# Two-layer decoder on one core: TensorE in place of DMA for the transpose of the attention weights, and three smaller re-orderings

## The chip, the cores and the metric

The kernel runs on one core of a Trainium2 chip. The metric is the device time of one execution in microseconds (us). TensorE (PE), VectorE (DVE), ScalarE (ACT), GpSimd (POOL) and SyncE (SP) each work through their own list of instructions in order and wait for each other by semaphores. SP only starts DMA transfers here. Matmul results land in PSUM, which the kernel divides into eight banks of 512 f32 values for each partition; DVE and ACT read them there.

## The reference, cut to what matters

Sixteen sequences of 128 tokens with 256 features (2048 rows in all) go through two decoder layers. Each layer is attention, cross attention and a feed-forward part, each with a residual and a layer norm.

```
x = layernorm(x + L0_attn(x))          # 16 heads of 128: local window and top-8 of compressed keys, out @ Wo + bo
x = layernorm(x + L0_xattn(x, ctx))    # 16 heads of 16, 2048 queries by 2048 keys, quantised
x = layernorm(x + L0_ffn(x))           # silu(gate) * up, 256 -> 1024 -> 256
x = layernorm(x + L1_attn(x))          # 32 heads of 8, causal inside a block of 128
x = layernorm(x + L1_xattn(x, ctx))    # 16 heads of 16, own sequence's context
x = layernorm(x + L1_ffn(x))           # 16 experts, top 6, and a shared expert

# L0_xattn, after the scores
attn = softmax(q @ k.T)                              # all 2048 keys of all sequences
attn = round(attn / (max/255)) clipped to 0..255     # an unsigned byte for each weight
out  = attn @ v @ Wp + bp
```

In the first attention the values have a bias: `lv = x @ Wlv + blv`, and the merged context is halved before `@ Wo`.

## The kernel before, in words

The stages run one after the other. By the profiled execution the first attention takes from the start to about 806 us, the preparation of the first cross attention to 879, its main loop (with the feed-forward part of the layer woven in) to 1618 and its tail to 1674, the second layer's attention to 1968, its cross attention to 2192, the experts to the end.

**First attention.** Steps are (block of 128 tokens, group of four heads), 64 in all, software-pipelined over four iterations: `normed` and `values` project (L355), `transposed` and `scores` follow one iteration later, `weightsT` two, `contexts` (L467) and `output` three. PE's order is written out by hand; a scheduler orders DVE, ACT and POOL. `contexts` ends with one ACT copy of four heads (L474, `mT`, scale 0.5). The bias `blv` is not added to the values: `output_bias` (L492), called once at n == 6, multiplies half of it by `Wo` with 16 matmuls of broadcast columns (POOL copies L497, PE L498), adds that to `bo` and adds `bo` to all 16 tiles `xs` (POOL, L501). SP loads the four `xT` groups first (L66), then `wcmp`, the tables, the weights, and the tiles `x` last.

**First cross attention.** A group `gp` is two query tiles, and a step is (gp, pair of heads i, tile u): 128 steps, 16 to a group, each of two parts. All engines are in an order written by hand. In each part PE makes the scores of 1024 keys for both heads (`scores`, L759, two tiles `s` of two banks from three buffers), DVE scales each and keeps the running maximum (`scaled`, L774, 128x1024 from PSUM). One step later ACT turns 2048 scores of one head into bytes with one exponential (`weights8`, L795; `snl` of L786 is its bias). The bytes are viewed as 16-bit words, and a DMA transpose on SP's queue (L803) brings the keys to the partitions. Two steps later POOL spreads the bytes to bf16 (`spread`, L807), and three to four steps later PE multiplies them with the values `vq` (`context`, L817). Because a word holds two keys, `values_by_key` (L651) lays the values out in the same order of two.

Beside it, `pair_work` and `due` place the queries of the next group (`query`; `query_cols` is a DMA transpose, L611), the division, the output projection, and the feed-forward part of the previous group: in steps 8 to 15 of a group the gate and up products (`ffn_gate`, L889), on ACT `ffn_out` (L907, L908) and `ffn_sigmoid` (L911).

**Second layer's attention.** Steps are (tile t, half c of the heads, quarter e), 64 in all; PE's order is written by hand. Keys of four heads are masked into one tile `kz` (POOL, L1253); `attend_scores` adds the causal mask with bf16 matmuls (L1261), then two products of 32 rows each, which lie in different row groups of PE (L1265), into one of two buffers `sc` of two banks; DVE takes the maximum (L1274) and subtracts it (L1276), ACT exponentiates (L1277). Two steps later PE transposes the weights (L1285) and ACT copies them (L1286); three steps later come the contexts (L1295) and the division (L1305). The projections (L1379), the values (L1388) and the output (L1324) share one PSUM tile `misc`.

Of the kernel before, what the change touches and what calls it, by code (L numbers as in the profile page):

```python
# [27 lines left out]
P = 128  # L28
# [20 lines left out]
def decoder(ctx: ExitStack, tc: tile.TileContext, w: dict, out: bass.AP):  # L49
# [15 lines left out]
    for g in range(NG):  # L65
        nc.sync.dma_start(out=xT[g], in_=xT_dram[:, :, g * G : (g + 1) * G])  # L66
# [125 lines left out]
    with ExitStack() as ph:  # L192
# [5 lines left out]
        nc.sync.dma_start(out=wcmp, in_=w["L0_attn_Wcmp"].rearrange("(k p) n -> p k n", p=P))  # L198
        rope_t = pool.tile([P, 4, 32], F32, name="rope_t")
# [23 lines left out]
        bo = load_row(pool, w["L0_attn_bo"], "bo0")  # L223
        for t in range(NB):
            nc.sync.dma_start(out=xs[t], in_=w["x"][t * P : (t + 1) * P, :])
# [241 lines left out]
        def contexts(b, st):  # L467

            pm = ps.tile([P, 4, P], F32, tag="pm", name="pm", bufs=1)
            for h in range(4):  # L470
                nc.tensor.matmul(pm[:, h, :], lhsT=st["Wlv"][:, h, :], rhs=st["plT"][:, h, :], start=True, stop=False)
                nc.tensor.matmul(pm[:, h, :], lhsT=cvz[b % 3][:, h, :], rhs=st["pcT"], start=False, stop=True)
            st["mT"] = wk.tile([P, 4, P], F32, tag="mT", name="mT")
            nc.scalar.activation(st["mT"], pm, AF.Copy, scale=0.5)  # L474
# [16 lines left out]

        def output_bias():  # L492

            pb = ps.tile([P, HID], F32, tag="po", name="pb", bufs=1)
            for h in range(NH):
                rep = wk.tile([P, P], F32, tag="blv_b", name="blv_b")
                nc.gpsimd.tensor_copy(rep, blv[:, h : h + 1].to_broadcast([P, P]))  # L497
                nc.tensor.matmul(pb, lhsT=rep, rhs=wts["Wo", h // 4][:, h % 4, :], start=h == 0, stop=h == NH - 1)  # L498
            nc.vector.scalar_tensor_tensor(bo, pb, 0.5, bo, ALU.mult, ALU.add)
            for t in range(NB):  # L500
                nc.gpsimd.tensor_tensor(xs[t], xs[t], bo, ALU.add)  # L501
# [7 lines left out]
        with tc.manual_schedule(engines={mybir.EngineType.PE}):  # L509
# [4 lines left out]
            for n in range(len(steps) + 6):  # L514
# [5 lines left out]
                if fourth:  # L520
                    contexts(fourth[0], fourth[2])
# [14 lines left out]
                if n == 6:  # L536
                    output_bias()
# [32 lines left out]
    with ExitStack() as ph:  # L570
# [40 lines left out]
        def query_cols(t):  # L611
            nc.sync.dma_start_transpose(out=qT[t % 4].bitcast(U16), in_=rows3.rearrange("p h d -> p (h d)").bitcast(U16))

        qs = {}
        with tc.tile_pool(name="l0x_1", bufs=1) as p1, tc.tile_pool(name="l0x_p0", bufs=2, space=PSUM) as ps0:
# [35 lines left out]
            def values_by_key(t4):  # L651
                pt = ps0.tile([P, 4, 2, P], BF16, tag="pt3", name="ptv")
                for i in range(4):
                    for c in range(2):
                        at = t4 * G + (i // 2) * 2 * P
                        keys = vqT[:, c, at : at + 2 * P].rearrange("p (w j) -> p j w", j=2)
                        nc.tensor.transpose(pt[:, i, c, :], keys[:, i % 2, :], ident16)
                nc.scalar.copy(vq[:, 4 * t4 : 4 * t4 + 4, :].rearrange("p t (c d) -> p t c d", c=2), pt)
# [49 lines left out]
            for n in range(NB + 4):  # L708
# [15 lines left out]
                if n in (7, 10):  # L724
                    query_cols(n // 10)
# [33 lines left out]
        def scores(gp, i, u, half, st):  # L759

            t = 2 * gp + u
            s = [ps.tile([P, 2, G], F32, tag="s", name="s", bufs=3) for _ in range(2)]
            for c in range(2):
                at = (2 * half + c) * G
                for hh in range(2):
                    r = slice(64 * hh, 64 * hh + 64)
                    nc.tensor.matmul(  # L767
                        s[hh][:, c, :], lhsT=qT[t % 4][r, i, :], rhs=kT[r, i, at : at + G], start=True, stop=True
                    )
            return s  # L770
# [17 lines left out]
        def weights8(gp, i, u, hh, st):  # L788
# [5 lines left out]
            a = wk.tile([P, 2 * G], U16, tag="a", name="a", bufs=3)  # L794
# [7 lines left out]
            at = wk.tile([P, 8, P], U16, tag="at", name="at", bufs=4)  # L802
            nc.sync.dma_start_transpose(out=at, in_=a)  # L803
            st["at"].append(at)

        def spread(u, hh, st, aT):
            nc.gpsimd.tensor_copy(  # L807
                aT[:, :, hh, u * P : (u + 1) * P].rearrange("p (b j) q -> p b j q", j=2),
                st["at"][hh].bitcast(U8).rearrange("p b (q j) -> p b j q", j=2),
            )  # L810
# [70 lines left out]
        def ffn_gate(q, i, n, tag="misc"):  # L881

            if n == 0:
                pp = ps.tile([P, 2, G] if tag == "s" else [P, 2, 2 * P], F32, tag=tag, name="gu", bufs=3 if tag == "s" else 1)
# [32 lines left out]
        def ffn_down_psum(tag="misc"):  # L917
            pp = ps.tile([P, 2, G] if tag == "s" else [P, G], F32, tag=tag, name="pd", bufs=3 if tag == "s" else 1)
# [30 lines left out]
        def query(t, at):  # L949
# [14 lines left out]
            later(at + 5, "SP", query_cols, t)  # L964
# [99 lines left out]
        ordered = [getattr(mybir.EngineType, nm) for nm in ("PE", "DVE", "Activation", "Pool", "SP")]  # L1064
        with tc.manual_schedule(engines=set(ordered)):
            for n in range(len(steps) + 9):
                now = steps[n] if n < len(steps) else None
                if now is not None:
                    if n % 16 == 0:
                        group(n // 16)  # L1070
                    if n < NB:
# [4 lines left out]
                        "at": [],  # L1076
                    }
                for part in range(2):
                    at = 2 * n + part
                    if now is not None:  # L1080
                        s = scores(*now, part, states[n])
                        scaled(*now, part, 0, states[n], s)
                        due(at, "DVE")
                        scaled(*now, part, 1, states[n], s)
                    else:
                        due(at, "DVE")
# [41 lines left out]
                    due(at, "SP")  # L1128
# [10 lines left out]
                states.pop(n - 2, None)  # L1139
# [116 lines left out]
    def attend_scores(wk, psum, qT, kz, blocks, mask):  # L1256

        sc = psum.tile([P, 2, 4, P], F32, tag="sc", name="sc", bufs=2)
        if mask is not None:
            for b in range(2):  # L1260
                nc.tensor.matmul(  # L1261
                    sc[:, b].rearrange("p j k -> p (j k)"), lhsT=ident16, rhs=mask, start=True, stop=False
                )
        for b, r in enumerate(blocks):
            nc.tensor.matmul(  # L1265
                sc[:, b].rearrange("p j k -> p (j k)"),
                lhsT=qT[r],
                rhs=kz[r].rearrange("p j k -> p (j k)"),
                start=mask is None,
                stop=True,  # L1270
            )
        sc = sc.rearrange("p b j k -> p (b j) k")
        mx = stat.tile([P, 8], F32, tag="amx", name="amx")
        nc.vector.tensor_reduce(mx, sc, AX.X, ALU.max)  # L1274
        pr = wk.tile([P, 8, P], F32, tag="pr", name="pr", bufs=3)
# [79 lines left out]
    with ExitStack() as ph:  # L1355
# [15 lines left out]
        cross_load()  # L1371
        moe_load()
        vs, qkT = {}, {}

        def project_a(g, n, c):

            pp = ps.tile([P, G], F32, tag="misc", name="proj")
# [16 lines left out]
        steps = [(t, c, e) for t in range(NB) for c in range(2) for e in range(2)]  # L1394
        kzs, prs, prTs, oTs = {}, {}, {}, {}
        with tc.manual_schedule(engines={mybir.EngineType.PE}):
            for n in range(2):
                for c in range(2):
                    project_a(0, n, c)
            values_a(0)  # L1400
            for n in range(len(steps) + 16):
                if n == 4:
                    cross_tables()

                if n in (5, 7):
                    q = NB // 2 - 2 + n // 7
                    norm_pair_xT(q, norm_pair_T(q, ps, "misc"))
                if n < len(steps):
                    t, c, e = steps[n]
                    cols = slice((t % 4) * P, (t % 4 + 1) * P)  # L1410
                    if e == 0:
                        kzs[c] = masked_keys(wk, qkT[t // 4, 1, c][:, cols], own1)
                    blocks = [slice(32 * i, 32 * i + 32) for i in (2 * e, 2 * e + 1)]
                    prs[n] = attend_scores(
                        wk, ps, qkT[t // 4, 0, c][:, cols], kzs[c], blocks, causal.rearrange("p j k -> p (j k)")
                    )
                if 0 <= n - 3 < len(steps):
                    t, c, e = steps[n - 3]
                    if e == 1:
                        attend_context([prTs.pop(n - 4), prTs.pop(n - 3)], vs[t], ones1, o2[:, c], 16 * c)  # L1420
                        oTs[t, c] = attend_divide(wk, o2[:, c])
                if 0 <= n - 2 < len(steps):
                    prTs[n - 2] = attend_transpose(wk, ps, prs.pop(n - 2))
                t, r = n // 4, n % 4
                if r == 0 and t // 4 + 1 < NG:
                    project_a(t // 4 + 1, t % 4 // 2, t % 2)
                elif r == 1 and t + 1 < NB:
                    values_a(t + 1)
                elif r == 3 and 0 <= t - 1 < NB:
                    attend_output(ps, t - 1, [oTs.pop((t - 1, c)) for c in range(2)], wz)  # L1430
                    if t % 4 == 0:
                        norm(t // 4 - 1)
                elif r == 2 and t // 4 >= 1 and t % 4 in (1, 2):
                    norm_T(t // 4 - 1, t % 4 - 1, ps, "misc")
# [4 lines left out]
    with ExitStack() as ph:  # L1439
# [51 lines left out]
        with tc.manual_schedule(engines={mybir.EngineType.PE}):  # L1491
# [8 lines left out]
            for n in range(len(steps) + 14):  # L1500
                if n < len(steps):
# [4 lines left out]
                    prs[n] = attend_scores(wk, ps, cols[t, 0][:, c, :], kzs.pop((t, c)), blocks, None)  # L1506
# [145 lines left out]
```

## Time and profile before

| | us |
|---|---|
| median of three runs (lowest, highest) | 2724.48 (2720.74, 2729.77) |
| the profiled execution's own time | 2727.17 |
| its span, first to last instruction | 2725.2 |
| outside the span | 2.0 |
| PE, DVE, ACT, POOL busy in the span | 2519.4, 1903.5, 1472.8, 1215.8 |
| first attention, 60 to 645: PE, DVE, ACT, POOL busy of 585 | 578.5, 453.0, 317.4, 288.2 |
| first cross attention, 878 to 1616: the same of 738 | 653.0, 688.9, 621.7, 618.9 |
| second layer's attention, 1676 to 1970: the same of 294 | 281.5, 212.5, 154.8, 90.1 |

Busy times of PE include the time in which results run out of its pipeline, so that a busy PE is not yet a full one. [...] In a row such as `L795 ACT ACTIVATE a<-e,snl ... x256 | 510.8, 1996 | 3.5` the numbers are the total busy time, the mean of one in nanoseconds, and the idle time of the engine just ahead of these instructions.

### The profile page before, as it was taken

To read this page: it belongs to the slowest core of one execution; us is meant where nothing else is said; L and a number is where in the kernel's file an instruction comes from. 1 tells how busy PE (TensorE), PEld (TensorE's weight loads), DVE (VectorE), ACT (ScalarE), POOL (GpSimd) and SP (SyncE) were. 2 spreads that over 40 slices of the span, in tenths; PEclk is the share of its full clock that TensorE was granted. 3 is DMA by queue.
4 is the path that set the end of the run, shared out by engine and by line. 5 is a ranking of instruction groups with operands and counts; after the bars stand their busy time and mean duration, and the time that the engine had idled before them with its cause. 6 is when DMAs were issued, how large, how long until landed. Compare 5 with 4: busy or idle time off the path is not lost. (4 is left out here: it accounts for less than half of the span.)

```text
span 2725.2 us, 39543 instructions
## 1 busy us (share of the span) xinstructions
PE 2519.4 (92%) x13877; PEld 1494.7 (55%) x13908; DVE 1903.5 (70%) x4365; ACT 1472.8 (54%) x2778; POOL 1215.8 (45%) x1336
## 2 busy tenths in 40 slices
PE   6999999999997788988988898999988899999998
PEld 3677777777764123433433345666655546564746
DVE  5677777877757999989999973777777742324232
ACT  3455555555543888977987873555554531313120
POOL 5544544444436888878888883223132200000000
PEclk9999999999998799999999999999999999999999
DMA  8000000000010566665665563100100011112120
GB/s 252 1 1 1 1 1 1 1 1 1 1 39 13 103 111 119 128 111 115 124 124 107 112 141 94 59 2 2 44 15 11 2 66 43 54 39 61 33 67 10
DMA packets 360150, 150.69 MB, mean 55 GB/s; under 512 B 294576, under 2 KB 341136, under 8 KB 359440
## 3 DMA queue, kind: packets, MB, share of 16 engines
q1 hardware_dynamic: 358592, 144.49, 22.9%
q0 software_dynamic: 1360, 3.68, 0.6%
q8 instruction: 110, 1.80, 0.3%
q14 instruction: 88, 0.72, 0.1%
HBM read 74.57 MB, written 2.23 MB: 28 GB/s over the span
## 5 line engine op out<-in xcount | busy, mean ns | idle before, releaser
L807 POOL CAST aT<-at 128x2048 bf16<-128x2048 uint8 x256 | 481.2, 1894 | 88.9 <-DMA at<-a 83.0
L795 ACT ACTIVATE a<-e,snl 128x2048 uint8<-128x2048 f32 x256 | 510.8, 1996 | 3.5
L774 DVE TENSOR_SCALAR_CACHE_REDUCE e<-s,qs,smx 128x1024 f32<-128x1024 f32 x256 | 335.2, 1335 | 14.7 <-PE s L767 13.9
L774 DVE TENSOR_SCALAR_CACHE_REDUCE e<-s,qs 128x1024 f32<-128x1024 f32 x256 | 319.9, 1281 | 33.8 <-PE s L767 28.8
L817 PE MATMUL o<-aT,vq 128*32 128x512 bf16 x1024 | 266.3, 395 | 3.3 <-POOL aT L807 3.3
L767 PE MATMUL s<-kT,qT 64*128 64x512 bf16 x1024 | 189.8, 399 | 30.0 <-DVE e L774 27.1
L1564 DVE TENSOR_TENSOR h<-h,up 128x512 f32<-128x512 f32 (+1 forms) x100 | 68.8, 688 | 192.4 <-PE up L1560 191.0
L1563 ACT ACTIVATE h<-gate 128x512 f32<-128x512 f32 (+1 forms) x100 | 59.7, 597 | 220.5 <-PE gate L1560 220.2
L817 PEld LDWEIGHTS <-vq 128*32 128x32 bf16 x1024 | 86.2, 98 | 165.5 <-issue 91.8
L1560 PE MATMUL gate<-xT,w_L_ffn_w1g 128*128 128x512 f32 x352 | 167.7, 595 | 0.0
L1560 PE MATMUL up<-xT,w_L_ffn_w1u 128*128 128x512 f32 x352 | 165.4, 592 | 0.0
L1274 DVE TENSOR_REDUCE amx<-sc 128x8 f32<-128x1024 f32 x96 | 116.7, 1216 | 62.4 <-PE sc L1265 62.2
L1591 PE MATMUL py<-w_L_ffn_w2T,h 128*128 128x256 f32 x704 | 154.6, 379 | 0.0
L1277 ACT ACTIVATE pr<-pr 128x1024 f32<-128x1024 f32 x96 | 101.6, 1059 | 88.3 <-DVE pr L1276 88.3
L1286 ACT COPY prT<-tp 128x512 f32<-128x512 f32 x192 | 104.3, 584 | 76.9 <-PE tp L1285 76.5
L1591 PEld LDWEIGHTS py<-w_L_ffn_w2T,h 128*128 128x128 f32 x704 | 133.7, 190 | 18.3
L889 PE MATMUL gu<-xT,wgu 128*128 128x256 f32 x448 | 132.3, 419 | 9.6 <-ACT gu_s L908 4.9
L425 ACT ACTIVATE pls<-sc,lm,rms_rs 128x128 f32<-128x128 f32 x256 | 113.8, 454 | 21.7 <-DVE lm L421 21.7
L355 PE MATMUL proj<-Wlk,xT 128*128 128x512 f32 x256 | 121.5, 597 | 3.0 <-ACT raw_Wlv L381 1.8
L482 PE MATMUL po<-Wo,mT 128*128 128x256 f32 x512 | 121.2, 380 | 1.4 <-ACT mT L474 1.4
L355 PE MATMUL proj<-Wq,xT 128*128 128x512 f32 x256 | 122.3, 601 | 0.2 <-DVE raw_Wlk L364 0.2
L1276 DVE TENSOR_TENSOR pr<-sc,amx 128x1024 f32<-128x1024 f32 x96 | 117.0, 1219 | 5.7
(313 smaller groups left out, 5383.5 us busy)
## 6 DMA issues: line engine op xcount, KB each, us to landing
wgu<-in_L_ffn_gu SPq DMA_DIRECT2D x112, 128.0 KB
sh<-share SPq DMA_DIRECT2D x32, 256.0 KB
at<-a SPq DMA_TRANSPOSE x256
sh<-share SPq DMA_DIRECT2D x16, 224.0 KB
sh<-share SPq DMA_DIRECT2D x16, 192.0 KB
w_L_ffn_w1g<-in_L_ffn_w1g SPq DMA_DIRECT2D x1, 2816.0 KB
w_L_ffn_w1u<-in_L_ffn_w1u SPq DMA_DIRECT2D x1, 2816.0 KB
w_L_ffn_w2T<-in_L_ffn_w2T SPq DMA_DIRECT2D x1, 2816.0 KB
```

Source lines behind the costliest of these rows:

```text
L355: nc.tensor.matmul(pp.rearrange("p h d -> p (h d)"), lhsT=xTt(b, k), rhs=wts[nm, hg][:, k, :], start=k == 0, stop=k == 1)
L482: nc.tensor.matmul(outs[b], lhsT=st["mT"][:, h, :], rhs=wts["Wo", hg][:, h, :], start=hg == 0 and h == 0, stop=hg == 3 and h == 3,)
L767: nc.tensor.matmul(s[hh][:, c, :], lhsT=qT[t % 4][r, i, :], rhs=kT[r, i, at : at + G], start=True, stop=True)
L774: nc.vector.tensor_scalar(st["e"][hh][:, half, :], s[hh].rearrange("p a b -> p (a b)"), qs[2 * gp + u][:, 2 * i + hh : 2 * i + hh + 1], No ...
L795: nc.scalar.activation(a.bitcast(U8), st["e"][hh].rearrange("p a b -> p (a b)"), AF.Exp, bias=st["nm"][:, hh : hh + 1], accum_out=groups[g ...
L807: nc.gpsimd.tensor_copy(aT[:, :, hh, u * P : (u + 1) * P].rearrange("p (b j) q -> p b j q", j=2), st["at"][hh].bitcast(U8).rearrange("p b ...
L817: nc.tensor.matmul(o[r : r + 32].rearrange("p a b -> p (a b)"), lhsT=vq[:, n, 32 * i : 32 * i + 32], rhs=aT[:, n].rearrange("p a b -> p (a ...
L889: nc.tensor.matmul(ffn_ps[q][:, n, :], lhsT=wt[:, k, :], rhs=xT[q // 2][:, k, at], start=k == 0, stop=k == 1)
L1274: nc.vector.tensor_reduce(mx, sc, AX.X, ALU.max)
L1276: nc.vector.tensor_tensor(pr, sc, bc(mx, 2, P), ALU.subtract)
L1560: nc.tensor.matmul(pp[:rows], lhsT=wt[:, k, :], rhs=xT[g][:, k, :], start=k == 0, stop=k == 1)
L1591: nc.tensor.matmul(py, lhsT=h[:rows, i4 * P : (i4 + 1) * P], rhs=wt, start=n == 0, stop=n == len(parts) - 1)
```

## The change

1. **Weights' words by TensorE.** `weights8` writes its bytes into a tile seen as 512 words of 32 bits. `words_T` transposes four blocks of 128 words on PE into PSUM, and `words_out` copies them to SBUF as 1024 elements of 16 bits: ACT does it, but for the first parts of steps 8 to 15 of a group, where DVE does it. `spread` and `values_by_key` now count four keys to a word. The scores' tiles `s` have two buffers in place of three; two banks go to the transposes. `query_cols` becomes eight PE transposes and an ACT copy.
2. **First attention.** Only `xT[0]` is loaded early, right after `wcmp`; the other three come after the weights and before `x`. `output_bias` is gone: ACT adds half of `blv` in the copies `mT`, one copy for each head, and POOL adds `bo` to each tile `x`.
3. **Second layer's attention.** A step is a half tile: four mask matmuls, then four products of 32 rows in four row groups, into both buffers `sc`; the order on ACT is written by hand too. The loads for the next stages are issued one step into the loop, and the first projections take the two transposes' buffers.

```diff
-    for g in range(NG):
+    def load_xT(g):
         nc.sync.dma_start(out=xT[g], in_=xT_dram[:, :, g * G : (g + 1) * G])
...
         nc.sync.dma_start(out=wcmp, in_=w["L0_attn_Wcmp"].rearrange("(k p) n -> p k n", p=P))
+        load_xT(0)
...
         bo = load_row(pool, w["L0_attn_bo"], "bo0")
+        for g in range(1, NG):
+            load_xT(g)
...
-            nc.scalar.activation(st["mT"], pm, AF.Copy, scale=0.5)
+            for h in range(4):
+                n = 4 * hg + h
+                nc.scalar.activation(st["mT"][:, h, :], pm[:, h, :], AF.Identity, bias=blv[:, n : n + 1], scale=0.5)
...
-                if n == 6:
-                    output_bias()
+                if n == 2:
+                    nc.vector.tensor_scalar_mul(blv, blv, 0.5)
+                if n % 4 == 2 and n // 4 < NB:
+                    nc.gpsimd.tensor_tensor(xs[n // 4], xs[n // 4], bo, ALU.add)
...
-            s = [ps.tile([P, 2, G], F32, tag="s", name="s", bufs=3) for _ in range(2)]
+            s = [ps.tile([P, 2, G], F32, tag="s", name="s", bufs=2) for _ in range(2)]
...
-            a = wk.tile([P, 2 * G], U16, tag="a", name="a", bufs=3)
+            a = wk.tile([P, G], F32, tag="a", name="a", bufs=4)
...
-            at = wk.tile([P, 8, P], U16, tag="at", name="at", bufs=4)
-            nc.sync.dma_start_transpose(out=at, in_=a)
-            st["at"].append(at)
+            st["a"].append(a)
+
+        def words_T(hh, st):
+            pt = ps.tile([P, 4, P], F32, tag="tp", name="aTp", bufs=2)
+            for b in range(4):
+                nc.tensor.transpose(pt[:, b, :], st["a"][hh][:, b * P : (b + 1) * P], ident)
+            return pt
+
+        def words_out(hh, st, pt, copy):
+            at = wk.tile([P, 4, P], F32, tag="at", name="at", bufs=3)
+            copy(at.bitcast(U16), pt.bitcast(U16))
+            st["at"][hh] = at
...
                     if now is not None:
                         s = scores(*now, part, states[n])
-                        scaled(*now, part, 0, states[n], s)
-                        due(at, "DVE")
-                        scaled(*now, part, 1, states[n], s)
-                    else:
-                        due(at, "DVE")
+                        for hh in range(2):
+                            scaled(*now, part, hh, states[n], s)
+                    due(at, "DVE")
+
+                    m = n - 2 + part
+                    if 0 <= m < len(steps):
+                        on_dve = m % 16 >= 8 and part == 0
+                        pt = words_T(1 - part, states[m])
+                        words_out(1 - part, states[m], pt, nc.vector.tensor_copy if on_dve else nc.scalar.copy)
+                    due(at, "PE")
...
-            later(at + 5, "SP", query_cols, t)
+            later(at + 5, "PE", lambda: box.update(T=query_cols(ps, "tp")))
+            later(at + 6, "ACT first", lambda: nc.scalar.copy(qT[t % 4], box["T"]))
...
+        scs = [psum.tile([P, 2, 4, P], F32, tag="sc", name="sc", bufs=2) for _ in range(len(blocks) // 2)]
+        banks = [sc[:, b].rearrange("p j k -> p (j k)") for sc in scs for b in range(2)]
         if mask is not None:
+            for bank in banks:
+                nc.tensor.matmul(bank, lhsT=ident16, rhs=mask, start=True, stop=False)
+        for bank, r in zip(banks, blocks):
...
+                if 0 < h < len(halves):
+                    scs = half_scores(t, c)
...
+                if 0 <= h - 2 < len(halves):
+                    u, d = halves[h - 2]
+                    attend_context([prTs.pop((h - 2, e)) for e in range(2)], vs[u], ones1, o2[:, d], 16 * d)
+                for e in range(2):
+                    if 0 <= h - 1 < len(halves):
+                        prTs[h - 1, e] = attend_transpose(wk, ps, prs.pop((h - 1, e)))
+                if h < len(halves):
+                    for e in range(2):
+                        prs[h, e] = attend_exp(wk, scs[e], 4)
```

## The prediction

> **What bounds the kernel now.** I read the page first, then the busy time of each engine by stage, then the groups of instructions, then the timeline of one step in each changed stage. The profiled execution took 2727.17 us, span 2725.2; it lies 2.7 above the median of the three runs, and my sum is made against 2727.
>
> PE is busy everywhere, but that is an average over stages with different limits.
>
> ```profile
> span 2725.2 us, 39543 instructions
> PE 2519.4 (92%) x13877; PEld 1494.7 (55%) x13908; DVE 1903.5 (70%) x4365; ACT 1472.8 (54%) x2778; POOL 1215.8 (45%) x1336
> ```
>
> In the first attention PE hardly waits: 578 of 585 us busy. In the loop of the first cross attention (879 to 1618, 738 us, 128 steps of 5.77) the stretches of one group each look like this (columns: stretch, its length, then busy time and instructions of PE, PEld, DVE, ACT, POOL, granted clock, DMA share, GB/s):
>
> ```profile
> 1155.00:1247.00 92.00, 83.28 (x372) 36.22 (x369) 83.48 (x141) 76.32 (x106) 75.96 (x67) 0.94 0.60 115
> 1247.00:1340.00 93.00, 84.60 (x384) 36.65 (x382) 86.44 (x147) 78.17 (x106) 79.62 (x71) 0.96 0.59 119
> ```
>
> Four engines at 82 to 93%: DVE is nearest to full, ACT has 15 us of 92 free. Steps 8 to 15 of a group, with the feed-forward work, take 5.36 us each, ACT back to back; steps 0 to 7 take 6.2. The groups that pay:
>
> ```profile
> L795 ACT ACTIVATE a<-e,snl 128x2048 uint8<-128x2048 f32 x256 | 510.8, 1996 | 3.5
> L774 DVE TENSOR_SCALAR_CACHE_REDUCE e<-s,qs,smx 128x1024 f32<-128x1024 f32 x256 | 335.2, 1335 | 14.7 <-PE s L767 13.9
> L774 DVE TENSOR_SCALAR_CACHE_REDUCE e<-s,qs 128x1024 f32<-128x1024 f32 x256 | 319.9, 1281 | 33.8 <-PE s L767 28.8 <-ACT snl L786 3.0 <-ACT gu_s L908 1.3
> L1276 DVE TENSOR_TENSOR pr<-sc,amx 128x1024 f32<-128x1024 f32 x96 | 117.0, 1219 | 5.7
> L706 ACT COPY kT<-pt 128x1024 bf16<-128x1024 bf16 x16 | 16.2, 1012 | 26.1 <-PE pt L705 26.1
> ```
>
> And the timeline, where I take hand-over times from (start, length, engine, line):
>
> ```profile
> 101.38 7.82 PE L498 MATMUL pb<-Wo,blv_b 128*128 128x256 f32 x28 [0.20 <-POOL blv_b L497]
> 109.74 11.75 POOL L501 TENSOR_TENSOR x<-x,bo 128x256 f32<-128x256 f32 x16 [1.30 <-DVE bo L499]
> 130.43 0.49 PE L471 MATMUL pm<-plT,raw_Wlv 128*128 128x128 f32 x2 [1.40 <-ACT plT L461]
> 132.54 0.49 PE L472 MATMUL pm<-pcT,cvz 128*128 128x128 f32 x2 [1.63 <-DVE pcT L465]
> ...
> 1198.34 2.00 ACT L795 ACTIVATE a<-e,snl 128x2048 uint8<-128x2048 f32 x1
> 1200.49 1.23 SPq L803 DMA_TRANSPOSE at<-a  x1
> ...
> 1804.20 0.86 PEld L1285 LDWEIGHTS tp<-ident,pr 128*128 128x128 f32 x8 [0.76 <-ACT prT L1286]
> 1804.89 1.07 ACT L1286 COPY prT<-tp 128x512 f32<-128x512 f32 x2 [0.31 <-PE tp L1285]
> ...
> 1815.49 0.59 PE L1261 MATMUL sc<-causal,ident 128*128 128x512 bf16 x2
> 1816.02 1.13 PE L1265 MATMUL sc<-kz,qkT 32*128 32x512 f32 x4
> 1817.07 1.08 PE L1295 MATMUL o<-prT,vz 128*32 128x128 f32 x32
> ```
>
> **The loop, on ACT.** The transposes leave SP's queue, where they cost no engine; 192 of 256 copies of 1024 16-bit elements come to ACT and 64 to DVE. The price is row L706, the same shape from PSUM: 1.01, and 0.98 from start to start. More than the copies counts their place. ACT's list is now copy, exponential, copy, exponential, and each copy needs the PE transpose of the exponential just before it. The chain of a part: from the start of an exponential until its bytes are released 2.13 (887.12 to 889.23 and 1198.34 to 1200.49), four transposes until ACT may start 0.70 (1804.20 to 1804.89), copy 0.98. Sum 3.81 for a part, 7.62 for a step. `snl` (0.30) fits in the wait of 0.8. In steps 0 to 7 both copies are ACT's: 61.0, and between copy and exponential two query copies (0.98) and copies of `ot` and `xT` (0.47 each): 63.9. In steps 8 to 15 one copy is DVE's: 2.13 + 0.70 + 0.98 + exponential 2.00 + the two reads of `gu` 0.73 + `snl` 0.33 = 6.87.
>
> **The loop, on DVE and PE.** With three buffers PE wrote half of the next scores while DVE still read. With two, the second head's tile is free only when DVE has done both: each part costs DVE's two readings and then PE's remaining products. The readings take 2.50 and 2.62 a part (1206.25 to 1208.75, 1208.93 to 1211.55); then 0.14 until PE starts (886.56 to 886.69), 0.64 from the scores to DVE (1218.92 to 1219.56): 0.78. A step is 5.12 + 1.56 = 6.68. In steps 8 to 15 DVE's copy fills one such gap. No 16-bit copy by DVE from PSUM is in the trace; the nearest rows, 1024 elements from PSUM, take 1.22 to 1.28, a copy of 128 takes 0.27. Between these I take 1.22, the row of that size: 6.68 + 0.44 = 7.12, longer than ACT's 6.87. The other end lies under the gap of 0.78 and leaves ACT's 6.87. In steps 0 to 7 DVE's other work (about 1.0 a step) sits in the gaps and ACT's 7.62 decides. PE's own work: eight transposes of 0.108 add 0.9 to about 4.5 a step, below either chain; but they stand in order ahead of the feed-forward and context products, which now wait for ACT with them. POOL's bytes come with another stride; I keep 1.89 (L807), two a step plus 1.5 of feed-forward, 5.3 of 7.
>
> Sum of a group: 63.9 + 8 x 7.12 = 120.9, before 92.2: +28.7, eight groups +229; the first group has less beside it: **+226**. Bounds: ACT's own instructions without a wait give steps of 6.29 with DVE's 6.68 over them, 53.4 + 57.0 a group, +146; all waits one behind the other, 8.2 a step (below), +335. I take the chain, as its order is fixed.
>
> Two rules of the Trainium skill can be weighed here. The rows price 1024 elements from PSUM at 1.22 on DVE; "VectorE: DVE Perf Modes", section "Why PSUM operands drop a tier", lets 16-bit data from PSUM run at two a cycle, an estimate of 0.66 by its table of costs; steps 8 to 15 would then take 6.87 and the sum would be 16 less. The rows show PE waiting only 27 us for DVE in this loop with three buffers; "Perfetto Trace Analysis", section "Matmuls", wants independent groups to rotate through banks so that the emptying of one overlaps the next, which speaks against the step from three to two: without that loss the sum would be smaller by the same 16, as ACT's chain stays.
>
> **First attention.** `output_bias` held PE from 98.95 to 109.03: -10.1. Its 16 additions kept POOL to 121.5, and PE lost 5.3 behind it (1.40, 1.63, and matmuls at half pace until 136): gone from there. At the start, PE now waits for 0.5 MB in place of 2 MB: in the trace `wcmp` came at 18.7, and 12 us of work lie from `lg` (23.4) to the next projection (35.5). By bytes at the measured 285 GB/s I expect a lead of 12.5. But the scheduler now puts the additions of `bo` on POOL in the third step, and they wait there for the tiles `x`, which land last: 14.1 of 17.1 MB, at about 49.5. Behind them stand `raw_Wlk` of that step and the next. POOL then needs 16 x 0.73 between its other work, until about 67, where PE's transposes would have been at 58.6: lead left 3 (0 to 12.5). The four `mT` copies cost ACT at most 4 x 0.454 (L425) against 0.59; PE needs them 2.6 after the contexts (59.68 to 62.28) and ACT is 54% busy: nothing, but 0.7 twice at the end, where nothing covers it. Sum **-18** (-8 to -28).
>
> **Second layer's attention.** PE sets the pace, 17.3 a tile. The scores of a quarter are 0.53 + 1.05, a half 3.16; four products side by side with four masks 0.95 + 1.05 = 2.00: -1.16. But the eight blocks of each quarter are now transposed in a row, four PSUM tiles from two buffers: the third waits for the first copy (0.70 + 0.58 + 0.1), so 2.35 in place of 1.72: +0.63. DVE is below: 4.96 for a half, 1.25 division, 0.5, and 1.8 until the next scores. A tile: 2 x -0.53 = -1.06, sixteen tiles -17; the first projections no longer share one buffer (1677.06 to 1685.09): -5. Sum **-22**. If the four products ran two by two, 2 x (-0.11 + 0.63) x 16 = +17 - 5 = +12; at DVE's pace of 14 a tile, -53.
>
> Total: 2727 + 226 - 18 - 22 = 2913, rounded to **2910**.
>
> **Rivals.**
> - *The wait is hidden.* PE's transpose overtakes, and ACT is held by its own work alone: +146 in the loop, 2833. For it: two PSUM buffers and four of `a`. Against: one list, one order.
> - *The waits add up.* In steps 8 to 15 PE stands at the scores for DVE and only then takes the words ACT waits for: 3.1 from scores to scores, 0.70, 0.98, then 2.00 + 0.73 + 0.33 and hand-overs, 8.2; the same in steps 0 to 7 with the extra copies: +335, about 3020. For it: PE is in order. Against: DVE's and ACT's cycles settle side by side when neither waits for the other's late half.
> - *Two by two.* The four products do not run together: 34 more, 2944.
> - *Not slower.* The DMA traffic (60% of the loop) is what held its engines, and they run faster without it. The loop must then take 778 at most, 6.08 a step: it decides from a chain shorter by 20%. Priced at that, 2720. Against: all 256 exponentials lie between 1985 and 2011 ns, with the queue full or empty, and DVE waits for PE, not for data.
>
> **How the numbers follow.** Forecast 0.58 (2850 to 2975), hidden 0.17, adding up 0.13, two by two 0.09, not slower 0.03. About 0.3% (8 us) is what a measurement can tell from no change. The range, 2825 to 2990, takes in most of the second and fourth case. Faster 0.03, same 0.01, slower 0.96.
>
> **What the profile after would show.** Right: the step near 7.6 in the first half of a group and 7.1 in the second; idle time of ACT ahead of the word copy, released by PE; that copy near 1.01; PE waiting for DVE ahead of the scores, several times the 27 us; `x` additions on POOL waiting for DMA at 45 to 55 us; the tile of the second layer's attention near 16.2. Wrong: ACT copies near 0.6, DVE or POOL fuller than ACT, or a stage outside these three that moves.

## The result, and the profile after

The changed kernel takes 2978.41 us (median of four runs, 2973.44 to 2978.68), before 2722.89. The ratio is 1.0929, with a 95% interval of 1.0906 to 1.0953. The predicted time was 2910, its range 2825 to 2990. The profiled execution's span grew from 2725.2 to 2976.6, by 251.4. From the traces' starts of a few instructions it splits like this:

| stretch | before | after | difference |
|---|---|---|---|
| start to the first exponential of the cross attention | 887.1 | 875.6 | -11.6 |
| first to last exponential of the loop | 733.9 | 995.8 | +261.9 |
| from there to the second layer's first projection | 56.1 | 59.1 | +3.0 |
| second layer's attention, to the first scores of its cross attention | 302.6 | 298.0 | -4.6 |
| the rest | 745.5 | 748.2 | +2.7 |

So the loop lost 265 with its drain, and the two small parts gave 16. On the page of the kernel after, PE, DVE and POOL have lost share, and ACT went only from 54% to 57%, though the work of ACT (+226) and PE (+151) grew much:

```profile
span 2976.6 us, 41945 instructions
PE 2670.3 (90%) x15028; PEld 1610.8 (54%) x15028; DVE 1950.6 (66%) x4429; ACT 1698.4 (57%) x3178; POOL 1212.8 (41%) x1320
```

The third and the fifth group of 16 steps, to be set beside the two stretches of before (columns: stretch, its length, busy time and instructions of PE, PEld, DVE, ACT, POOL, granted clock, DMA share, GB/s):

```profile
1120.80:1246.00 125.20, 104.39 (x533) 51.55 (x533) 93.14 (x157) 103.87 (x134) 80.83 (x71) 0.99 0.06 18
1373.50:1499.30 125.80, 105.78 (x533) 51.91 (x533) 93.11 (x157) 103.87 (x134) 80.81 (x71) 0.97 0.06 17
```

A group takes 125 in place of 92. DVE was busy 83 of 92 and 86 of 93 us; now it is busy 93 of 125. No engine is above about 84%, and the DMA share fell from 0.60 to 0.06. As nothing is full, I looked for a chain of waits. The groups of instructions say which one (idle time ahead of each, and its releasers, last):

```profile
L795 ACT ACTIVATE a<-e,snl 128x2048 uint8<-128x2048 f32 x256 | 513.6, 2006 | 1.9
L774 DVE TENSOR_SCALAR_CACHE_REDUCE e<-s,qs 128x1024 f32<-128x1024 f32 x256 | 318.8, 1282 | 171.1 <-PE s L767 152.1
L774 DVE TENSOR_SCALAR_CACHE_REDUCE e<-s,qs,smx 128x1024 f32<-128x1024 f32 x256 | 333.6, 1341 | 91.3 <-PE s L767 91.3
L813 ACT COPY at<-aTp 128x1024 uint16<-128x1024 uint16 x192 | 194.3, 1012 | 176.0 <-PE aTp L807 167.4
L807 PE MATMUL aTp<-ident,a 128*128 128x128 f32 x1024 | 177.5, 298 | 106.5 <-ACT a L795 106.1
L767 PE MATMUL s<-kT,qT 64*128 64x512 bf16 x1024 | 193.4, 398 | 31.7 <-DVE e L774 30.3
```

ACT's wait stands ahead of the word copy (176.0), hardly ahead of the exponential (1.9); its releaser is PE's transpose, and where PE waits ahead of the transposes (106.5), the releaser is the exponential just before. DVE waits 243 us for PE's scores, before 43. The timeline of ACT in steps 0 to 7 of a group shows the bare beat:

```profile
1251.30 2.00 ACT L795 ACTIVATE a<-e,snl 128x2048 uint8<-128x2048 f32 x1
1253.29 0.28 ACT L786 ACTIVATE snl<-smx,ln 128x2 f32<-128x2 f32 x1
1254.19 1.01 ACT L813 COPY at<-aTp 128x1024 uint16<-128x1024 uint16 x1 [0.62 <-PE aTp L807]
1255.10 2.00 ACT L795 ACTIVATE a<-e,snl 128x2048 uint8<-128x2048 f32 x1
1257.99 1.01 ACT L813 COPY at<-aTp 128x1024 uint16<-128x1024 uint16 x1 [0.80 <-PE aTp L807]
1258.90 2.00 ACT L795 ACTIVATE a<-e,snl 128x2048 uint8<-128x2048 f32 x1
```

From 1251.30 to 1258.90 two parts in a row (the second of step 0 and the first of step 1) take 7.60, where the forecast chain is 7.62. That it fits this closely is partly luck: from an exponential to its copy are 2.89 (1255.10 to 1257.99) against 2.83, from the copy to the next exponential 0.91 against 0.98. And it accounts for a step only when PE comes in time. The next part, on PE:

```profile
1257.25 0.66 PE L807 MATMUL aTp<-ident,a 128*128 128x128 f32 x4 [0.47 <-ACT a L795]
1257.74 0.61 PE L612 MATMUL ptq<-ident,rows 128*128 128x128 bf16 x8
1258.28 1.47 PE L827 MATMUL o<-aT,vq 128*32 128x512 bf16 x6
1259.68 1.56 PE L934 MATMUL pd<-w_L_ffn_d,h 128*128 128x256 f32 x6
1261.17 0.61 PE L767 MATMUL s<-kT,qT 64*128 64x512 bf16 x4
1261.71 0.66 PE L807 MATMUL aTp<-ident,a 128*128 128x128 f32 x4
```

ACT's exponential of 1258.90 was over at about 1261.0. Its transposes start at 1261.71, because query rows, contexts, a down product and the next scores stand ahead of them in PE's order. In groups 1 to 6, 42 of the 48 steps 0 to 7 take 8.1 to 10.5, one 7.8, and only five 7.6.

### The profile page after: what moved, and what is told of

It is laid out like the page before. It is cut to its first block, busy times and chain, and to the rows that moved or that the text cites. A ratio compares the mean times of both kernels' runs of the same rounds, so it can differ in the third digit from the quotient of the medians.

```text
span 2976.6 us, 41945 instructions
## 1 busy us (share of the span) xinstructions
PE 2670.3 (90%) x15028; PEld 1610.8 (54%) x15028; DVE 1950.6 (66%) x4429; ACT 1698.4 (57%) x3178; POOL 1212.8 (41%) x1320
## 3 DMA queue, kind: packets, MB, share of 16 engines
q8 instruction: 119, 1.95, 0.3%
## 5 line engine op out<-in xcount | busy, mean ns | idle before, releaser
L795 ACT ACTIVATE a<-e,snl 128x2048 uint8<-128x2048 f32 x256 | 513.6, 2006 | 1.9
L813 ACT COPY at<-aTp 128x1024 uint16<-128x1024 uint16 x192 | 194.3, 1012 | 176.0 <-PE aTp L807 167.4
L807 PE MATMUL aTp<-ident,a 128*128 128x128 f32 x1024 | 177.5, 298 | 106.5 <-ACT a L795 106.1
L807 PEld LDWEIGHTS aTp<-ident,a 128*128 128x128 f32 x1024 | 113.7, 147 | 234.5 <-ACT a L795 201.7
L1265 POOL TENSOR_TENSOR vz<-v,ones 128x1024 f32<-128x1024 f32 (+1 forms) x32 | 58.4, 1826 | 202.0 <-ACT v L1402 83.3
L899 PE MATMUL gu<-xT,wgu 128*128 128x256 f32 x448 | 124.7, 402 | 13.8 <-ACT xT L161 11.5
```

The costliest lines, as they stand in the source:

```text
L795: nc.scalar.activation(a.bitcast(U8), st["e"][hh].rearrange("p a b -> p (a b)"), AF.Exp, bias=st["nm"][:, hh : hh + 1], accum_out=groups[g ...
L807: nc.tensor.transpose(pt[:, b, :], st["a"][hh][:, b * P : (b + 1) * P], ident)
L813: copy(at.bitcast(U16), pt.bitcast(U16))
L899: nc.tensor.matmul(ffn_ps[q][:, n, :], lhsT=wt[:, k, :], rhs=xT[q // 2][:, k, at], start=k == 0, stop=k == 1)
```

## The experiments

All figures by group are means over the groups 1 to 6 of the loop, from the starts of the exponentials: before 49.3 for steps 0 to 7 and 43.9 for steps 8 to 15, after 70.0 and 55.5. Where "one run" is said, the kernel has a single time, so that differences under 10 us between such kernels are not read.

### The loop of before with the two small parts

```diff
-            s = [ps.tile([P, 2, G], F32, tag="s", name="s", bufs=2) for _ in range(2)]
+            s = [ps.tile([P, 2, G], F32, tag="s", name="s", bufs=3) for _ in range(2)]
...
-        def words_T(hh, st):
...
+            nc.sync.dma_start_transpose(out=at, in_=a)
+            st["at"].append(at)
...
```

> The changed kernel with the first cross attention of before (DMA transposes of words and query rows, three buffers s), the other two parts kept. My theory, from the profile after: the loop and its drain cost 264 of the 251 by which the span grew, the first attention gives 10.9 and the second layer's attention 4.7. This kernel should take 2727 - 11 - 5 = about 2711 by the profiled execution, 2704 to 2716. Rival 1: part of the 264 comes from the other two parts (the moved loads, another fill of the loop); then it stays at or above 2720. Rival 2: the small parts give what was forecast, 18 and 22; then about 2687.

Measured: 2709.03 against 2723.82, ratio 0.9948 (0.9932 to 0.9964). The gain is 15, the 16 of the stretches and not the forecast 40. The small parts are worth what their stretches show, and all of the loss lies in the loop.

### Two buffers for the scores, and nothing else

```diff
-            s = [ps.tile([P, 2, G], F32, tag="s", name="s", bufs=3) for _ in range(2)]
+            s = [ps.tile([P, 2, G], F32, tag="s", name="s", bufs=2) for _ in range(2)]
```

> The kernel before with two buffers s in place of three and nothing else changed (two banks lie idle). By the sum of the prediction each part costs DVE's two readings and 0.78 until the next scores: 6.68 a step in place of 5.36 in steps 8 to 15 and of 6.2 in steps 0 to 7, the loop at least 855 in place of 738, the total about 2840 (2820 to 2860). Rival: PE waited only 27 us for DVE in this loop, and the scores come early enough with two buffers: 0 to 20 more, 2725 to 2745.

One run: 2860.11, so +136, at the upper end of what was expected. Half of the loop's loss needs no transpose and no copy. The groups of DVE and of PE's scores in this run (idle time was 14.7 and 33.8 before on DVE, and PE waited 27 for DVE):

```profile
L774 DVE TENSOR_SCALAR_CACHE_REDUCE e<-s,qs,smx 128x1024 f32<-128x1024 f32 x256 | 335.4, 1336 | 72.9 <-PE s L767 72.9
L774 DVE TENSOR_SCALAR_CACHE_REDUCE e<-s,qs 128x1024 f32<-128x1024 f32 x256 | 320.1, 1282 | 95.4 <-PE s L767 93.9 <-ACT xT L160 1.5
L767 PE MATMUL s<-kT,qT 64*128 64x512 bf16 x1024 | 240.6, 403 | 130.9 <-DVE e L774 126.5 <-ACT kT L706 1.1
```

Steps 8 to 15 take 50.4, 6.3 a step, a little under the 6.68 of two readings and a gap of 0.78: the gaps are 0.5 to 0.7. Steps 0 to 7 take 58.3, 7.3 a step. There the prediction let DVE's other work sit in the gaps, and it does not. The timeline shows why: PE makes one product of the next scores, waits for DVE, makes the other three, and only after them takes contexts and a down product, which then stand between DVE and the scores after these:

```profile
1218.78 0.37 PE L767 MATMUL s<-kT,qT 64*128 64x512 bf16 x1 [0.26 <-DVE e L774]
1219.99 0.59 PE L767 MATMUL s<-kT,qT 64*128 64x512 bf16 x3 [0.83 <-DVE e L774]
1220.51 1.47 PE L817 MATMUL o<-aT,vq 128*32 128x512 bf16 x6
1222.16 1.56 PE L924 MATMUL pd<-w_L_ffn_d,h 128*128 128x256 f32 x6 [0.19 <-DVE x L857]
1223.65 1.01 PE L767 MATMUL s<-kT,qT 64*128 64x512 bf16 x4
```

### The copy behind the next exponential

Only ACT's list differs from the changed kernel.

```diff
-                        words_out(1 - part, states[m], pt, nc.vector.tensor_copy if on_dve else nc.scalar.copy)
+                        if on_dve:
+                            words_out(1 - part, states[m], pt, nc.vector.tensor_copy)
...
                         weights8(*steps[n - 1], part, states[n - 1])
+                    if 0 <= m < len(steps) and not on_dve:
+                        words_out(1 - part, states[m], pt, nc.scalar.copy)
```

> The changed kernel where only ACT's list differs: the copy of a part's words stands behind the next exponential and no longer ahead of it (PE's order and POOL's lag are as in the changed kernel). Theory of the chain exponential, transposes, copy, next exponential: it is broken here, ACT's list goes through without a wait, and what is left is the loss from two buffers s (2860 alone) and PE's transposes: 2860 to 2890. Rival, occupancy of ACT or PE's order: nothing is taken away, 2960 to 2990.

One run: 2892.81, 86 less than the changed kernel and 3 above the range expected of the chain, with the same instructions. The groups of ACT:

```profile
L795 ACT ACTIVATE a<-e,snl 128x2048 uint8<-128x2048 f32 x256 | 512.0, 2000 | 3.0
L813 ACT COPY at<-aTp 128x1024 uint16<-128x1024 uint16 x192 | 192.0, 1000 | 24.0 <-PE aTp L807 23.3 <-POOL np_rstd L143 0.3 <-issue 0.2
```

ACT's wait ahead of the copies went from 176 to 24. A group takes 62.7 + 52.0. So what the place of the copies in ACT's list costs is shown: 86, of which about 58 in steps 0 to 7 and 28 in steps 8 to 15. Neither ACT's occupancy nor PE's order alone held the changed kernel, since neither was touched here.

### The words one part later, twice

```diff
-                    m = n - 2 + part
+                    m = n - 2
...
-                        pt = words_T(1 - part, states[m])
-                        words_out(1 - part, states[m], pt, nc.vector.tensor_copy if on_dve else nc.scalar.copy)
+                        pt = words_T(part, states[m])
+                        words_out(part, states[m], pt, nc.vector.tensor_copy if on_dve else nc.scalar.copy)
```

> The changed kernel, with each word transposed and copied one part later, so that the copy ahead of an exponential needs the exponential before the last one and not the last one. Theory of the chain: ACT no longer waits; its own list gives 0.91 + 2.09 for a part, 6.3 a step with snl, in steps 8 to 15 with the reads of gu about 6.2; DVE and PE with two buffers s give 5.12 + 1.56 = 6.7. A group goes from 125.5 to about 108, the total from 2978 to about 2850 (2830 to 2880). Rival, PE's order: transposes stand behind the other products (a part of PE's work is 3.95 in the steps with pd), so nothing is gained: 2960 or more. Rival, occupancy: ACT's work alone sets the pace; as no work is taken away, the time stays at 2978.

One run: 2940.17, an expectation missed. Steps 8 to 15 did fall, from 55.5 to 51.5, but steps 0 to 7 rose to 71.1. PE waited there for POOL's query rows, which are made behind a spread that now waits longer:

```profile
1121.50 0.62 PE L612 MATMUL ptq<-ident,rows 128*128 128x128 bf16 x8 [1.85 <-POOL rows L605]
```

The second kernel also moved the transposes of these rows by two parts.

```diff
-            later(at + 5, "PE", lambda: box.update(T=query_cols(ps, "tp")))
-            later(at + 6, "ACT first", lambda: nc.scalar.copy(qT[t % 4], box["T"]))
+            later(at + 7, "PE", lambda: box.update(T=query_cols(ps, "tp")))
+            later(at + 8, "ACT first", lambda: nc.scalar.copy(qT[t % 4], box["T"]))
```

> The run with words one part later took 2940: steps 8 to 15 fell from 6.88 and 7.17 to 6.28 and 6.59, but steps 1, 4 and 5 rose to 8.4 to 12.3, where PE waited up to 2 us for the query rows that POOL made later. Here the query rows are also transposed two parts later. Theory: that wait goes, steps 0 to 7 take about 7.2 as with two buffers s alone, a group 110 to 114, total 2870 to 2900. Rival: the lag itself makes POOL late for the contexts, PE stands there instead, and the total stays above 2925.

One run: 2914.94, between the two theories: 25 less, steps 0 to 7 at 68.0. The wait for the rows is gone, and the transposes no longer wait for the exponential, but ACT still waits for the transposes:

```profile
L813 ACT COPY at<-aTp 128x1024 uint16<-128x1024 uint16 x192 | 194.3, 1012 | 121.9 <-PE aTp L807 118.4 <-POOL np_rstd L143 1.9
L807 PE MATMUL aTp<-ident,a 128*128 128x128 f32 x1024 | 177.0, 298 | 1.5 <-ACT a L795 1.5
```

Against the changed kernel, ACT's wait for PE ahead of the copies fell from 4.9 to 1.0 a group in steps 8 to 15, but only from 15.3 to 14.1 in steps 0 to 7. In steps 8 to 15 the lag does break the chain from exponential to exponential (51.6). In steps 0 to 7 the transposes are late behind PE's other work, and an exponential that stands behind a copy is late with them; the copy one place later in ACT's list frees the exponential from both. The rival's cause does not show: POOL waited 178 us for ACT's copies between 1000 and 1750 (83 in the changed kernel), but PE's contexts waited for POOL's bytes 1.0 us in all.

### All copies on DVE

```diff
-                        words_out(1 - part, states[m], pt, nc.vector.tensor_copy if on_dve else nc.scalar.copy)
+                        words_out(1 - part, states[m], pt, nc.vector.tensor_copy)
```

> The changed kernel with all 256 word copies on DVE, where one took 0.69 in the profile after (1.01 on ACT). Theory of the chain: ACT's list has no copy that waits for PE any more; DVE is then the fullest, 5.12 + 2 x 0.69 = 6.5 a step and about 1.0 of other work in steps 0 to 7, so 7.0 to 7.5 in steps 0 to 7 and 6.6 to 7.0 in steps 8 to 15: a group of 109 to 116, the total 2880 to 2920. Rival, occupancy of ACT: 192 x 0.91 = 175 go, total about 2800. Rival, PE's order: no gain, 2960 or more.

One run: 2887.13, 91 less than the changed kernel, in the range of the chain's theory; a group takes 62.5 + 52.8. Taking 192 copies of about 0.91 each, 175 us of work, off ACT gives no more than moving them in its list (86). By itself this does not price the copies' sum on ACT, as DVE is now nearly full: in the fourth group it is busy 107 of 115 us, ACT 83 (columns as above).

```profile
1209.19:1324.62 115.43, 101.56 (x535) 51.09 (x532) 107.12 (x180) 82.69 (x110) 81.02 (x71) 1.00 0.07 19
```

### The transposes alone

The kernel with two buffers, in which PE also transposes the words, for nobody; the words still come by DMA.

```diff
+        def words_T(hh, st):
+            pt = ps.tile([P, 4, P], F32, tag="tp", name="aTp", bufs=2)
+            for b in range(4):
+                nc.tensor.transpose(pt[:, b, :], st["a"][hh][:, b * P : (b + 1) * P], ident)
...
+                    m = n - 2 + part
+                    if 0 <= m < len(steps):
+                        words_T(1 - part, states[m])
```

> The kernel before with two buffers s (2860), and PE also transposes each part's words at the place where the changed kernel does it, in its own two PSUM tiles, but nobody reads the result: the words still come by DMA. This prices the transposes' place in PE's order without any copy. The changed kernel without its chain (copy behind the next exponential) took 2893, and its small parts give about 15, so 48 us beside the two buffers are unexplained. Theory: they are PE's, whose transposes wait for the exponential with the feed-forward and context products queued behind them; this run then takes 2890 to 2910. Rival: the copies cost them, on DVE and through the later bytes for POOL; then the transposes fill idle time of PE, 2860 to 2870.

One run: 2888.46, 28 more than with two buffers alone, nearly all in steps 8 to 15 (50.4 to 53.5; steps 0 to 7 58.3 to 58.8). So 28 of the 48 are PE's. The other 20 are a remainder of single runs of three kernels, no more than an order of size, and not shown to be the copies': the kernels also differ in the transposes of the query rows, in DVE's order and in POOL's bytes.

### The additions of bo behind the attention's output

On the kernel with the loop of before.

```diff
-                if n % 4 == 2 and n // 4 < NB:
-                    nc.gpsimd.tensor_tensor(xs[n // 4], xs[n // 4], bo, ALU.add)
+                if n == 2:
+                    nc.gpsimd.tensor_tensor(xs[NB - 1], xs[NB - 1], bo, ALU.add)
...
                 nc.vector.tensor_tensor(xs[b], xs[b], outs.pop(b), ALU.add)
+                if b < NB - 1:
+                    nc.gpsimd.tensor_tensor(xs[b], xs[b], bo, ALU.add)
```

> The kernel with the loop of before and the two small parts, but each addition of bo to a tile x on POOL comes behind DVE's addition of the attention's output to that tile (the last tile's stays early). In the profile after the additions held POOL at 55.7 to 71.5 us and PE lost 1.7 and 2.5 waiting for pls and pcT, its second output products were 7.4 late, its first 1.1. Theory: 4 to 6 of that come back, 2709 becomes about 2704. Rival: the tiles and weights arrive late because of the order of the loads, and POOL's additions only fill that wait; then no change, 2707 to 2711.

Measured: 2706.29 against 2726.47, ratio 0.9925 (0.9896 to 0.9954), to be set beside 0.9948 (0.9932 to 0.9964). By the total alone that is inconclusive, as the intervals overlap. By the stage it is not: the loop's first scores come at 860.8 in place of 866.1, 5.3 earlier, of which the unchanged loop and its drain lost 4 again (1.3 are left at the second layer's first projection; single steps of the loop differ by up to 1.5 both ways). The three longest waits of PE between 56 and 160, of the kernel with the early additions:

```profile
PE pm L477 <- DVE pcT L469: 2.7, 2, 2.5
PE tp_p L463 <- POOL pls L457: 1.7, 1, 1.7
PE proj L359 <- DVE ck L327: 0.4, 1, 0.4
```

and all of them with the later ones:

```profile
PE proj L359 <- DVE ck L327: 0.7, 1, 0.7
PE proj L359 <- ACT raw_Wlv L385: 0.2, 1, 0.2
```

### The contexts between the two groups of transposes

On the kernel just shown.

```diff
-                if 0 <= h - 2 < len(halves):
-                    u, d = halves[h - 2]
-                    attend_context([prTs.pop((h - 2, e)) for e in range(2)], vs[u], ones1, o2[:, d], 16 * d)
                 for e in range(2):
                     if 0 <= h - 1 < len(halves):
                         prTs[h - 1, e] = attend_transpose(wk, ps, prs.pop((h - 1, e)))
+                    if e == 0 and 0 <= h - 2 < len(halves):
+                        u, d = halves[h - 2]
+                        attend_context([prTs.pop((h - 2, i)) for i in range(2)], vs[u], ones1, o2[:, d], 16 * d)
```

> As the run with the later additions, and in the second layer's attention the contexts' 64 products stand between the two groups of transposes. Theory: PE's wait of 0.24 to 0.29 for the copy ahead of the second group goes, with the matmuls' drain up to 0.4 a half tile, 32 times: 8 to 13 less, about 2693 where the other is 2704. Rival: DVE's chain (maximum, subtraction, division) sets the half tile's pace with 16.4 to 17.8 a tile, and PE only waits elsewhere: 0 to 3 less.

Measured: 2689.21 against 2726.47, ratio 0.9869 (0.9852 to 0.9887). The stage takes 282.6 in place of 296.0. On PE's timeline the changed kernel has

```profile
2086.58 1.09 PE L1299 MATMUL tp<-ident,pr 128*128 128x128 f32 x8
2087.97 1.14 PE L1299 MATMUL tp<-ident,pr 128*128 128x128 f32 x8 [0.29 <-ACT prT L1300]
2088.95 1.03 PE L1400 MATMUL proj_v<-w_L_attn_WvT,xT 128*128 128x256 f32 x4
```

2.37 for both groups, and this one

```profile
1807.78 1.10 PE L1283 MATMUL tp<-ident,pr 128*128 128x128 f32 x8
1808.80 1.08 PE L1293 MATMUL o<-prT,vz 128*32 128x128 f32 x32
1809.70 1.06 PE L1293 MATMUL o<-prT,ones 128*32 128x128 f32 x32
1810.69 1.09 PE L1283 MATMUL tp<-ident,pr 128*128 128x128 f32 x8
1811.62 1.03 PE L1384 MATMUL proj_v<-w_L_attn_WvT,xT 128*128 128x256 f32 x4
```

1.02 + 0.93 = 1.95: 0.42 less, 32 times, is 13.4, all that the stage gave. This kernel is the fastest of the study: the loop of before, and the two small parts with their orders mended.

## Why the prediction was right, and where not

**Sign, stage and range** were right, and the mechanism that I gave, the place of the copies in ACT's list, is there and is worth 86 of the loss. It does not set the pace of most steps 0 to 7, though, and the range held by its wide upper end: 2978 is 3 above the upper end of the forecast case (2975). Two parts of the bare chain, 7.62, were measured as 7.60, the copy (1.01 by row L706) as 1.012. The sum was 68 short of 2978; these are the terms.

**The loop, forecast +226 (146 to 335), measured 265.** Steps 0 to 7: 63.9 forecast, 70.0 measured. The step that failed is "PE's own work ... below either chain". That PE has time on average is true, it waits 106 us for exponentials; but contexts, down products and query rows stand between its scores and the transposes, and where they sum to more than the chain leaves, the transposes are late. I had priced a late PE only in the rival in which the waits add up, and there by its wait for DVE, which is small. Steps 8 to 15: 57.0 forecast, 55.5 measured, as the copy on DVE takes 0.69 and not 1.22: half of these steps take 6.87 to 6.90, ACT's cycle of 6.87 that I had put below DVE's. That too high price hid 12 of the 49 us by which steps 0 to 7 were short, which is luck.

**What the loss is made of.** I took the larger of two cycles, ACT's and that of DVE and PE. By my own bounds (+146 without ACT's waits, +226 with them) the chain was to add 80, and moving the copies took off 86. I also said that without the loss of a buffer the sum would be only 16 smaller; no run shows that, as the chain was not run with three buffers. By single runs, one edit after the other, the loss is 136 for the buffer, 28 for the transposes in PE's order, 86 for the copies' place in ACT's list, and a remainder of about 20 (with the 16 of the small parts taken off, about the whole 255). These are steps along one path; another order of the edits could share them out otherwise. The cycle of the two buffers alone is no small one: 58.3 + 50.4 = 108.7 a group, where my formula gives 16 x 6.68 = 106.9. As a maximum it was hidden behind 120.9; the changed kernel's 125.5 lies above both. That the two cycles delay each other on PE is my reading, not shown apart.

**The two pages weighed.** DVE's copy of 1024 16-bit elements from PSUM:

```profile
L813 DVE COPY at<-aTp x64: 684/689/692, 951.7 to 1874.7; 128x1024 uint16<-128x1024 uint16 x64
```

0.689 is near the 0.66 estimated from the Trainium skill, "VectorE: DVE Perf Modes", section "Why PSUM operands drop a tier"; my row of equal size had f32 operands and was the wrong neighbour. "Perfetto Trace Analysis", section "Matmuls", wants groups to rotate through banks; giving up one of three buffers cost 136 us here. The 27 us that PE waited for DVE before were no measure of the third buffer's worth.

**First attention, forecast -18, measured -11.6.** The bias products gave 11.4 (-10.1 forecast; PE's lag against before goes from 7.4 late to 4.0 early across them) and the stall behind them 5.2 (-5.3). The step that failed is the start's lead, which I kept at 3 and bounded by zero. PE's first product did come 13.8 earlier (5.8 against 19.6), but its second step's keys wait for their weights and the entries for the chain through ACT, POOL and DVE: the keys' products start at 27.3 against 29.6 and take 3.75 in place of 1.96, and the entries' last start at 35.46 in both. After the change:

```profile
5.76 3.75 PE L299 MATMUL pl<-xT,wcmp_b 128*128 128x512 f32 x4 [5.76 <-DMA xT<-in_xT]
27.29 3.75 PE L359 MATMUL proj<-Wlk,xT 128*128 128x512 f32 x4 [5.21 <-DMA Wlk<-in_L_attn_Wlk]
35.46 0.79 PE L323 MATMUL pk<-w_L_attn_Wk,entT 128*128 128x128 f32 x2 [2.53 <-DVE entT L318]
```

Then POOL's additions made the first output products 1.1 and the second 7.4 late. That the additions would hold POOL's queue was seen; that they leave a loss and not a lead was not. They did not wait for the tiles' loads, as I had it: they ran from 55.7 to 71.5 between POOL's other work. The run with the later additions gave 5 of that back.

**Second layer's attention, forecast -22, measured -4.6.** The four products do run together: they take 1.14, where two took 1.13 before (the trace has two rows for each), and with the masks a half tile's scores take 2.03 (from 2082.67 to 2084.70; forecast 2.00):

```profile
2082.67 1.03 PE L1278 MATMUL sc<-causal,ident 128*128 128x512 bf16 x4
2083.62 1.14 PE L1280 MATMUL sc<-kz,qkT 32*128 32x512 f32 x8
2084.70 1.08 PE L1309 MATMUL o<-prT,vz 128*32 128x128 f32 x32
```

The transposes take 2.37 (2.35 forecast). But tiles 4 to 12 take 16.97 on average against 17.49, half of the forecast 1.06: undisturbed tiles are at 16.4, others at 16.7 to 17.0, and those in which DVE's normalisation of four tiles (2.1 us) stands ahead of the maximum at 17.8. And the first tile takes 16.2 in place of 11.0, as it fills by halves, while the first products wait 4.5 for `kz` on POOL, so that the projections' own buffers gave 1.5 and not 5.

**The signs I named:** idle time ahead of the copies and copy time came as said. The step did so in the second half of a group (6.9 on average, 7.1 forecast) but not in the first (8.75, not 7.6). PE's wait for DVE ahead of the scores, forecast at several times 27, was 30: with the chain in place DVE waits for PE (243) and not PE for DVE; with two buffers alone it was 126. The additions to `x` did not wait for DMA, and the tile of the second layer took 17.0, not 16.2.

**Rivals.** "The wait is hidden" (2833) is excluded by ACT's 176 us of idle time ahead of the copies and by the 86. "Not slower" is excluded by the time; the exponentials took 2006 ns with the DMA share at 0.06, against 1996 before. "Two by two" did not occur. "The waits add up" (3020, 8.2 a step) comes near most of the steps 0 to 7 in size (8.1 to 10.5) but not in cause, as PE waited for DVE only 2 us a group there, and it fits none of the steps 8 to 15.

## What to carry to other kernels

An instruction that waits for another engine's answer to the instruction just before it belongs behind the next independent one in an in-order list: the same copies one place later were worth 86 us. A PSUM buffer is priced by a run with one fewer and not by the waits that show while it is there: PE waited 27 us for DVE with three, and going to two cost 136. An engine with time to spare on average can still be late in its order: PE's other work brought steps 0 to 7 to 70.0, where the larger of the two cycles gave 63.9.

## What was not expected of the hardware

DVE copies 1024 16-bit elements from PSUM in 0.69 us, ACT in 1.01, while for f32 operands of 1024 elements from PSUM DVE took 1.22 to 1.34. Three buffers together with the transposes were not tried: the kernel gives out all eight banks (six for the scores in that case, one each for `o` and `misc`), and the transposes need some. Whether the chain would also cost 86 with three buffers stays open.
